# Row transfers of a mixture-of-experts layer paced by the tile, and moved inside the attention before it

## The chip, the cores and the metric

The kernel runs on one core of a Trainium2 chip. A core has five engines that run on their own and wait for each other by semaphores: TensorE (PE in the profile; its weight loads are shown as PEld), VectorE (DVE), ScalarE (ACT), GpSimd (POOL) and SyncE (SP), which here only issues transfers. Transfers move data between the core's on-chip memory and DRAM. Those with addresses taken from a table (indirect ones) are issued by GpSimd, all the others in this part by SyncE. Each engine and each issuing queue works in the order in which its instructions stand.

The metric is the device time of one execution in microseconds, as the median of several runs.

## The reference

Eight layers in a row, each followed by a residual addition and a layer norm: four attentions and four feed-forward networks ("ffn"), on a state of 8 blocks of 256 tokens with 256 features (seen as 2 x 128 or 4 x 64 tokens by some layers). Only the last two are touched.

The last attention, cut to its core (16 heads, two score maps each, their difference normalized again):

```python
energy = jnp.einsum('bqhad,bkhad->bahqk', qd, kd)
energy = jnp.where(causal, NEG, energy)
scores = jax.nn.softmax(energy / np.sqrt(D), axis=-1)
diff = scores[:, 0] - lam * scores[:, 1]
diff = jax.nn.softmax(jnp.where(causal, NEG, diff), axis=-1)
att = jnp.einsum('bhqv,bvhd->bqhd', diff, v)
```

The last ffn is a mixture of 32 experts; each token goes to the four with the largest routing weight:

```python
routing_weights = jax.nn.softmax(router_logits, axis=-1)
top_k_weights, top_k_indices = jax.lax.top_k(routing_weights, 4)
top_k_weights = top_k_weights / top_k_weights.sum(axis=-1, keepdims=True)
gate_up = jnp.einsum('TD,EDF->TEF', x, gate_up_proj)
g, u = jnp.split(gate_up, 2, axis=-1)
next_states = jnp.einsum('TEF,EFD->TED', u * jax.nn.silu(g), down_proj)
next_states = (next_states * router_weights[..., None]).sum(axis=1)
```

The kernel computes for each token only its four experts.

## The kernel before

**The last attention** (`attn3`, L537 to L847) works through 48 units: a block, a half of its 128-row query tiles, and one or two heads of each of four groups. A loop (L818) runs them as a pipeline with one unit in each stage. Its body, in the order in which it hands out instructions:

- `factors` of the unit before (L652): DVE takes reciprocals of the sums; GpSimd masks the diagonal of the first softmax (L661) and makes the factor `c` (L666, L667);
- a step of the queue `others` (L830);
- `scores` of this unit (L618): PE products, DVE maxima `nm` (L643), ACT exponentials `e` (L646);
- `values` of the unit three back, and steps of the next block's projections;
- `differences` of the unit before (L671), in two halves: DVE combines the two maps (`e`, L680, with `c`) and takes the maximum `nmd` (L684); GpSimd scales `nmd` (L685) and makes `v` (L688);
- a second step of `others` (L842);
- `turned` of the unit two back (L694): PE transposes its `v` (L705), ACT takes the exponential `p` (L707).

**The queue `others`** holds one generator, `ffn3_sort` (L1877), put there when the fourth block is normed (L799). It routes the first group of tokens of the next layer (the tokens come in two groups of four blocks, `GROUPS`): logits, top four, a slot for every pair of token and expert (`place`, L850), and then `scatter` (L931): 32 indirect transfers issued by GpSimd, each of 128 token rows of 1 KB from `X` to their slots in the DRAM tensor `rows` of the group. Between steps the generator yields. Behind the transfers it yields after two of three (L1923), so that a step issues one or two.

**The last ffn** (`ffn3`, L2037) runs `ffn3_experts` once for each group. The sorted rows are cut into 63 tiles of 128, each belonging to one expert (L31). For tile j the pipeline of L1996 does, one iteration each: `turn` (PE transposes the rows `xg`, DVE copies them to `xTg`), `up` (PE product with the expert's gate and up weights, ACT `sg`, DVE product `h`), `turn_back` (PE transposes `h`, ACT copies it to `hT`), and eight iterations after `turn` (`LAG`) `down` (PE product, ACT copy to `yg`). The expert's number is read into a register of PE. SyncE fetches three tiles of rows at a time, six tiles ahead (`fetch`, L1934, four buffers), and stores three tiles of results to the DRAM tensor `outs` (L1987, two buffers of `yg`). SyncE's order in this part is laid out by a scheduler's own model; the four computing engines keep the order in which the code hands out instructions.

While the first group's tiles run, `ffn3` works off what the attention left (L2054: one step every three tiles) and then one step a tile of `ffn3_sort` for the second group, with its 32 row transfers. While the second group's tiles run, it takes one step a tile of `ffn3_combine` (L2003) for the first group: for each 128 tokens, four indirect gathers of 128 result rows from `outs` into `yk` by GpSimd (L2019), four multiply-adds on DVE (`rk`, L2025, two 128-token tiles behind the gathers), and for every two tiles the norm: moments on DVE, `rsq` and `rstd` on GpSimd (L145, L146), the normalization on DVE (L189), and the store of the block. When all tiles are done, `ffn3_combine` runs for the second group with nothing beside it.

Of the kernel before, what the change touches and what calls it, by code (L numbers as in the profile page):

```python
# [10 lines left out]
F32 = mybir.dt.float32  # L11
# [7 lines left out]
P = 128  # L19
# [14 lines left out]
LAG = 8  # L34
# [5 lines left out]
class Model:  # L40


    def __init__(self, ctx, tc, ins, out):
        self.tc, self.nc, self.ins, self.out = tc, tc.nc, ins, out
        nc = self.nc
        self.const = ctx.enter_context(tc.tile_pool(name="const", bufs=1, side="left"))
        self.small = ctx.enter_context(tc.tile_pool(name="small", bufs=4, side="left"))
        self.psum = ctx.enter_context(
            tc.tile_pool(name="psum", bufs=2, space=bass.MemoryType.PSUM)
        )  # L50
        self.n_ev = 0
        self.rows, self.outs = (
            [
                nc.dram_tensor(f"{x}{g}", (n * P, D), F32, kind="Internal").ap()
                for g, n in enumerate(TILES)
            ]
            for x in ("rows", "outs")
        )
        self.lrows, self.louts = (
            [  # L60
                nc.dram_tensor(f"{x}{g}", (n * P, d), F32, kind="Internal").ap()
                for g, n in enumerate(TILES0)
            ]
            for x, d in (("lrows", ROW0), ("louts", P))
        )
        self.left = []
        self.sorted, self.sorted0 = {}, {}

        c = self.const
        self.X = [c.tile([P, 2, D], F32, name=f"X{b}", tag=f"X{b}") for b in range(NB)]  # L70
        self.xT = [c.tile([P, 2, BLK], F32, name=f"xT{k}", tag=f"xT{k}") for k in range(NBLK)]
        self.ident = c.tile([P, P], F32, name="ident")
        nc.sync.dma_start(out=self.ident, in_=ins["c_ident"])
        self.load_x(0, 2)

        self.tri = c.tile([P, 2 * P], F32, name="tri")
        self.identb = c.tile([P, P], BF16, name="identb")
        nc.vector.tensor_copy(self.identb, self.ident)
        self.maskA = c.tile([P, 4, P], BF16, name="maskA")
        self.one32 = c.tile([P, 32], F32, name="one32")  # L80
        nc.vector.memset(self.one32, 1.0)
        self.nhalf = c.tile([P, 16], F32, name="nhalf")
        nc.gpsimd.memset(self.nhalf, -0.5)
# [453 lines left out]
    def attn3(self, w, act, keep, start=False, beside=None):  # L537
# [5 lines left out]
        nc = self.nc  # L543
# [258 lines left out]
        others = []  # L802
# [15 lines left out]
        for n in range(len(units) + 3):  # L818

            def at(back):  # L820
                return units[n - back] if 0 <= n - back < len(units) else None

            u, last = at(0), at(1)
            if u and u.qc == 0 and u.h0 == 0:
                step(projections, 100)
                if u.b + 1 < NB:
                    projections.append(project(u.b + 1))
            if last:
                last.factors()
            step(others)  # L830
            if u:
                u.scores()
            if at(3):
                at(3).values()
            step(projections)
            halves = last.differences() if last else iter(())
            next(halves, None)
            step(projections, 2 if u and u.qc == 0 else 1)
            step(ends)
            next(halves, None)  # L840
            next(halves, None)
            step(others)  # L842
            if at(2):
                at(2).turned()
            ends += done
            done.clear()
# [1027 lines left out]
            gup=self.load(pool, "f3_gup", [P, 32, 2, 192], split=8),  # L1874
        )

    def ffn3_sort(self, w, g, act):  # L1877

        nc = self.nc
        first, n = GROUPS[g]
        n *= 2
        lg = self.ps("t")[:, : n * 32].rearrange("p (t e) -> p t e", e=32)
        for t in range(n):
            for c in range(2):
                nc.tensor.matmul(
                    lg[:, t, :], self.xt(first + t // 2, t % 2, c), w["gate"][:, c, :],
                    start=(c == 0), stop=(c == 1),  # L1890
                )
        nm = act.tile([P, n], F32, tag="r_nm", name="r_nm", bufs=1)
        nc.vector.tensor_reduce(nm, lg, AX.X, ALU.max)
        pr = act.tile([P, n, 32], F32, tag="r_pr", name="r_pr", bufs=1)
        nc.vector.tensor_tensor(
            pr, lg, nm.unsqueeze(2).to_broadcast([P, n, 32]), ALU.subtract
        )
        nc.scalar.activation(pr, pr, AF.Exp)
        yield
        top = act.tile([P, n, 8], F32, tag="r_top", name="r_top", bufs=1)  # L1900
        idx = act.tile([P, n, 8], U32, tag="r_idx", name="r_idx", bufs=1)
        for t in range(n):
            nc.vector.max(top[:, t, :], pr[:, t, :])
            nc.vector.max_index(idx[:, t, :], top[:, t, :], pr[:, t, :])
            if t % 4 == 3 or t == n - 1:
                yield
        one, slots, ends = yield from self.place(w, act, self.const, f"f3{g}", idx[:, :, 0:4], n)
        rows = self.scatter(
            self.rows[g], slots, lambda t, k: self.X[first + t // 2][:, t % 2, :]
        )  # L1910
        next(rows)
        expert = yield from self.tile_experts(w, act, self.const, f"f3{g}", ends)

        wt = self.const.tile([P, n, 4], F32, tag=f"r_w{g}", name="r_w", bufs=1)
        sm = act.tile([P, n], F32, tag="r_sm", name="r_sm", bufs=1)
        nc.vector.tensor_reduce(sm, top[:, :, 0:4], AX.X, ALU.add)
        nc.vector.reciprocal(sm, sm)
        nc.vector.tensor_tensor(
            wt, top[:, :, 0:4], sm.unsqueeze(2).to_broadcast([P, n, 4]), ALU.mult
        )  # L1920
        self.sorted[g] = wt, slots, expert
        yield
        for i, _ in enumerate(rows):  # L1923
            if i % 3 != 0:
                yield

    def ffn3_experts(self, w, g, act):


        nc = self.nc  # L1930
# [23 lines left out]
        def up(j):  # L1954
            er[j] = nc.tensor.value_load(expert[0:1, j : j + 1], min_val=0, max_val=31)
            ps = self.ps("a")[:, :192]
            for c in range(2):
                nc.tensor.matmul(  # L1958
                    ps, xT[j][:, c, :], w["gup"][:, bass.ds(er[j], 1), c, :].rearrange(
                        "p o f -> p (o f)"  # L1960
                    ),
                    start=(c == 0), stop=(c == 1),
                )
            sg = act.tile([P, 96], F32, tag="sg", name="sg", bufs=3)
            nc.scalar.activation(sg, ps[:, 0:96], AF.Silu)
            h[j] = act.tile([P, 96], F32, tag="h", name="h", bufs=3)
            nc.vector.tensor_tensor(h[j], sg, ps[:, 96:192], ALU.mult)

        def turn_back(j):
            pt = self.ps("s")[:96, :P]  # L1970
# [22 lines left out]
        fetch(3)  # L1993
        if self.down is None:
            self.down = self.load(act, "f3_down", [96, 32, D], split=8)
        steps = ((0, turn), (1, up), (2, turn_back), (LAG, down))  # L1996
        for j in range(tiles + LAG):
            for i, f in steps:
                if 0 <= j - i < tiles:
                    f(j - i)  # L2000
            yield

    def ffn3_combine(self, g, act):  # L2003


        nc = self.nc
        first, n = GROUPS[g]
        wt, slots, _ = self.sorted[g]
        ys, rs = {}, {}
        for t in range(2 * n + 2):  # L2010
            i = t - 2
            b = first + i // 2
            if t < 2 * n:
                ys[t] = act.tile([P, 4, D], F32, tag="yk", name="yk", bufs=4)
# [22 lines left out]
    def ffn3(self, w, act, left, start=False):  # L2037
# [20 lines left out]
        for x in left:  # L2058
            for _ in x:
                pass  # L2060
        put = self.ffn3_combine(0, act)
        for _ in self.ffn3_experts(w, 1, act):
            next(put, None)
        for _ in put:
            pass
        for _ in self.ffn3_combine(1, act):
            pass


# [1 line left out]
def tile_layers(ctx: ExitStack, tc: tile.TileContext, ins, out, phases):  # L2071
    m = Model(ctx, tc, ins, out)
    sides = ("left", "right")
    stack = {}
# [23 lines left out]
    for i, name in enumerate(phases):  # L2098
        m.last = i == len(phases) - 1
        with tc.tile_pool(name=f"act{i}", bufs=2, side=sides[i % 2]) as act:  # L2100
# [4 lines left out]
            with tc.manual_schedule(engines=engines) if name in MANUAL else ExitStack():  # L2105
# [10 lines left out]
                elif name == "attn1":  # L2116

                    def then(i=i):
                        keeps[i - 1].close()
                        open_weights(i + 1)  # L2120

                    m.attn1(w, act, left, then, start=start)
                elif name == "attn3":
                    beside = None
                    if not m.last:
                        beside = partial(m.ffn3_sort, stack[i + 1][1], 0)
                    left = m.attn3(w, act, kept[i], start=start, beside=beside)
                elif name == "ffn3":
                    m.ffn3(w, act, left, start=start)
                    keeps[i - 1].close()  # L2130
                else:
                    getattr(m, name)(w, act, start=start)
# [126 lines left out]
```

## Time and profile before

| | us |
|---|---|
| median of 3 runs (2551.92 to 2557.06) | 2555.08 |
| the profiled execution | 2616.84 |
| its span | 2615.1 |
| PE busy in the span | 2245.8 |
| DVE busy | 1433.7 |
| ACT busy | 1043.8 |
| GpSimd busy | 891.6 |

The profile is of one execution. The last attention lasts from about 1775 to 2253 us in it, the tiles of the first group from 2258 to 2421, those of the second from there to 2554, and the rest is the last combine. Time is given from the start of the span. A transfer that GpSimd issues is shown as an instruction of GpSimd; those of SyncE are shown as SPq. In a timeline, the bracket says how long the engine was idle before the instruction and what ended that; "remote" is a release that the profile cannot name. The sum of the engines' busy times says little here, since the stages have different limits.

### The profile page before, as it was taken

The numbers are of one execution on the slowest core, as the hardware profiler recorded it, in microseconds if no ns is written. First come the engines' busy times: TensorE is split into PE (matmuls) and PEld (weight loads), VectorE is DVE, ScalarE is ACT, GpSimd is POOL, SyncE is SP. The second block draws the span as 40 slices with busy tenths as digits, with TensorE's granted clock in tenths as the row PEclk, the third lists the DMA queues.
The fourth block names the chain that finished last, engine by engine and source line by source line (L and its number), as shares of the span: only waits on it lengthen the run. The fifth ranks groups of instructions, "written<-read, shape, count | busy, mean of one in ns | idle before, by whom it ended". The sixth has DMA issues, their size and how long they took to land.

```text
span 2615.1 us, 35980 instructions
## 1 busy us (share of the span) xinstructions
PE 2245.8 (86%) x12016; PEld 1522.2 (58%) x12016; DVE 1433.7 (55%) x3597; ACT 1043.8 (40%) x3001; POOL 891.6 (34%) x1599
## 2 busy tenths in 40 slices
PE   8998889899999999999999999898877866677790
PEld 4554688756666666666654565455555644455570
DVE  4655286754544544543474354656888886442353
ACT  1233355453543543534431112214776556433240
POOL 1222234343433332332222220004666558431315
PEclk9998999999999999999999999998989887788795
DMA  5000411100001000000520101002000001434453
GB/s 153 1 1 1 154 37 45 45 20 4 4 3 35 17 1 1 1 1 1 196 73 0 49 1 50 1 1 99 1 1 1 2 9 41 119 125 148 148 161 98
DMA packets 92306, 120.74 MB, mean 46 GB/s; under 512 B 9757, under 2 KB 79582, under 8 KB 91102
## 3 DMA queue, kind: packets, MB, share of 16 engines
q1 hardware_dynamic: 82270, 95.75, 11.4%
q0 software_dynamic: 8192, 21.11, 2.5%
q8 instruction: 100, 1.64, 0.3%
q10 hardware_dynamic: 1664, 1.57, 0.2%
q14 instruction: 80, 0.66, 0.1%
HBM read 67.53 MB, written 50.88 MB: 45 GB/s over the span
## 4 chain that ended last, share of the span: by engine, by line
PE 25%; DVE 11%; POOL 7%; issue 3%; ACT 2%; DMA 1%; another core or an unknown queue 1%; POOLq 0%; SPq 0%; DVEq 0%; ACTq 0%
PE ps_a L1958 4%; DVE e L680 2%; PE ps_a L1579 2%; PE ps_o L1977 2%; PE ps_s L1579 2%; POOL v L688 2%; PE ps_o L1830 2%; PE ps_a L1783 2%; PE ps_s L1783 2%; DVE nm L643 1%; DVE nmd L684 1%; POOL yk L2019 1%; PE ps_t L1950 1%; DVE bnst L182 1%; POOL rows L937 1%
## 5 line engine op out<-in xcount | busy, mean ns | idle before, releaser
L1370 POOL TENSOR_SCALAR p<-p,rs 128x128 f32<-128x128 f32 (+1 forms) x256 | 104.2, 424 | 293.6 <-DVE rs L1368 289.2
L145 POOL TENSOR_SCALAR rsq<-bnmv 128x2 f32<-128x2 f32 x64 | 13.7, 214 | 516.3 <-DVE bnmv L183 508.9
L1360 ACT ACTIVATE p<-ps_s,nm,rq 128x128 f32<-128x128 f32 (+1 forms) x256 | 127.9, 506 | 151.2 <-DVE nm L1358 151.1
L1288 ACT ACTIVATE sq<-ps_a 128x512 f32<-128x512 f32 x126 | 76.0, 603 | 227.9 <-PE ps_a L1280 227.7
L1958 PE MATMUL ps_a<-w_f_gup,xTg 128*128 x504 | 119.2, 363 | 40.8 <-DVE xTg L1952 20.8
L646 ACT ACTIVATE e<-ps_a,nm 128x128 f32<-128x128 f32 (+1 forms) x256 | 105.8, 436 | 110.9 <-DVE nm L643 95.6
L688 POOL TENSOR_SCALAR v<-e,r,nmd 128x128 f32<-128x128 f32 (+1 forms) x256 | 135.4, 540 | 10.0
L1289 DVE TENSOR_REDUCE ssk<-sq 128x4 f32<-128x512 f32 x64 | 43.8, 686 | 172.4 <-ACT sq L1288 172.4
L1280 PE MATMUL ps_a<-w_a_wq,xT 128*128 128x512 f32 x256 | 123.6, 606 | 11.7 <-DVE k L1302 9.2
L705 PE MATMUL ps_t<-ident,v 128*128 128x128 f32 x384 | 69.9, 319 | 69.0 <-DVE qT L584 31.4
L680 DVE SCALAR_TENSOR_TENSOR e<-e,c 128x128 f32<-128x128 f32 (+1 forms) x256 | 106.1, 463 | 34.6 <-POOL c L667 34.4
L1280 PE MATMUL ps_a<-w_a_wv,xT 128*128 128x512 f32 x256 | 121.4, 596 | 2.1 <-ACT q L1313 2.1
L1958 PEld LDWEIGHTS ps_a<-w_f_gup,xTg 128*128 128x128 f32 x504 | 88.4, 210 | 53.0 <-issue 28.5
L1280 PE MATMUL ps_a<-w_a_wk,xT 128*128 128x512 f32 x248 | 116.5, 593 | 0.0
L1289 DVE TENSOR_REDUCE ssq<-sq 128x4 f32<-128x512 f32 x64 | 43.9, 686 | 131.9 <-ACT sq L1288 131.9
L1408 PE MATMUL ps_o<-w_a_wo,attT 128*128 128x256 f32 x512 | 111.8, 379 | 0.0
L646 ACT ACTIVATE e<-ps_s,nm 128x128 f32<-128x128 f32 (+1 forms) x256 | 106.8, 453 | 0.0
L1408 PEld LDWEIGHTS ps_o<-w_a_wo,attT 128*128 128x128 f32 x512 | 96.7, 190 | 12.8
L705 PEld LDWEIGHTS ps_t<-ident,v 128*128 128x128 f32 x384 | 50.2, 163 | 89.4 <-POOL nmd L685 44.9
L1144 DVE SCALAR_TENSOR_TENSOR yg<-ps_t,xg,yg 128x128 f32<-128x128 f32 x266 | 93.0, 350 | 13.6 <-PE ps_t L1133 2.9
L1347 PE MATMUL ps_s<-kT,qT 128*128 128x256 f32 (+1 forms) x512 | 99.5, 327 | 0.0
L2019 POOL DMA_INDIRECT yk<-outs,r_slots x64 | 62.2, 973 | 108.3 <-DMA outs<-yg 89.9
(402 smaller groups left out, 6127.5 us busy)
## 6 DMA issues: line engine op xcount, KB each, us to landing
rows<-zero SPq DMA_DIRECT2D x42, 384.0 KB
xg<-rows SPq DMA_DIRECT2D x42, 384.0 KB
outs<-yg SPq DMA_DIRECT2D x42, 384.0 KB
w_f_gup<-in_f_gup SPq DMA_DIRECT2D x8, 768.0 KB
w_f_w<-in_f_w SPq DMA_DIRECT2D x8, 512.0 KB
w_f_down<-in_f_down SPq DMA_DIRECT2D x8, 384.0 KB
w_f_up<-in_f_up SPq DMA_DIRECT2D x5, 512.0 KB
lrows<-zero SPq DMA_DIRECT2D x12, 204.0 KB
```

Of the source, the lines that this page charges most:

```text
L646: nc.scalar.activation(e[:, s, j * nk : (j + 1) * nk], sc[s][:, j, :], AF.Exp, bias=nm[:, s, j : j + 1], scale=1.0, accum_out=sums[:, s, j ...
L680: nc.vector.scalar_tensor_tensor(d[:, s, h, :], u.e[:, s, h, 1, :], u.c[:, s, h : h + 1], d[:, s, h, :], ALU.mult, ALU.add,)
L688: nc.gpsimd.tensor_scalar(u.v[:, s, h, :], d[:, s, h, :], u.r[:, s, h, 0:1], nm[:, s, h : h + 1], ALU.mult, ALU.add,)
L705: nc.tensor.transpose(ps[:, s, c, :], x, self.ident)
L1280: nc.tensor.matmul(ps, self.xt(u.b, t, c), w[which][:, c, u.cols], start=(c == 0), stop=(c == 1),)
L1347: nc.tensor.matmul(sc[:, j, :], u.qT[:, h0 + j, qc * P : (qc + 1) * P], u.kT[:, h0 + j, 0:nk], start=(j == 0), stop=False,)
L1360: nc.scalar.activation(u.p[qc][:, h0 + j, :], sc[:, j, :], AF.Exp, bias=nm[:, j : j + 1], scale=r[:, j : j + 1], accum_out=u.sums[qc][:, h ...
L1370: nc.gpsimd.tensor_scalar(u.p[qc][:, j, :], u.p[qc][:, j, :], ri[:, j : j + 1], 1.0, ALU.mult, ALU.mult,)
L1408: nc.tensor.matmul(y[:, t, :], attTs[b][:, h, t * P : (t + 1) * P], w["wo"][:, h, :], start=(h == 0), stop=(h == 15),)
L1579: nc.tensor.matmul(x, xT[:, c, tok], w[name][:, c, cols], start=(c == 0), stop=(c == 1),)
L1783: nc.tensor.matmul(x, w[name][:, c, cols], xT[:, c, :], start=(c == 0), stop=(c == 1))
L1958: nc.tensor.matmul(ps, xT[j][:, c, :], w["gup"][:, bass.ds(er[j], 1), c, :].rearrange("p o f -> p (o f)"), start=(c == 0), stop=(c == 1),)
```

## The change

Six edits, all for the last two layers:

1. In the attention's loop, the second step of `others` (behind the differences) becomes two steps, but is left out while `ffn3_sort` is at its row transfers (a flag, `scattering`).
2. `ffn3_sort` yields after each row transfer, or, in the attention, after every third (`each=3`). Those of the first group so stand three in a row behind the factors.
3. Each `up` gets a copy of one element of `h` on GpSimd (`beat`): GpSimd's queue cannot pass it before that tile's `h` is there. `h` has four buffers instead of three. With one step of the sort a tile, one transfer stands between two beats.
4. In the second group `down` comes four iterations after `turn`, instead of eight.
5. `ffn3_combine` of the first group starts at the second group's iteration 8 instead of 0, with one step, so at most one gather, an iteration.
6. The last `ffn3_combine` lets its multiply-adds trail the gathers by one 128-token tile instead of two.

```diff
             next(halves, None)
             next(halves, None)
-            step(others)
+            if not self.scattering:
+                step(others, 2)
...
-    def ffn3_sort(self, w, g, act):
+    def ffn3_sort(self, w, g, act, each=1):
...
         self.sorted[g] = wt, slots, expert
+        self.scattering = True
         yield
         for i, _ in enumerate(rows):
-            if i % 3 != 0:
+            if i % each == each - 1:
                 yield
+        self.scattering = False
...
-            h[j] = act.tile([P, 96], F32, tag="h", name="h", bufs=3)
+            h[j] = act.tile([P, 96], F32, tag="h", name="h", bufs=4)
             nc.vector.tensor_tensor(h[j], sg, ps[:, 96:192], ALU.mult)
+
+            beat = act.tile([1, 1], F32, tag="beat", name="beat", bufs=2)
+            nc.gpsimd.tensor_copy(beat, h[j][0:1, 0:1])
...
         if self.down is None:
             self.down = self.load(act, "f3_down", [96, 32, D], split=8)
-        steps = ((0, turn), (1, up), (2, turn_back), (LAG, down))
-        for j in range(tiles + LAG):
+            lag = LAG
+        else:
+            lag = 4
+        steps = ((0, turn), (1, up), (2, turn_back), (lag, down))
+        for j in range(tiles + lag):
...
-    def ffn3_combine(self, g, act):
+    def ffn3_combine(self, g, act, ahead):
...
-        for t in range(2 * n + 2):
-            i = t - 2
+        for t in range(2 * n + ahead):
+            i = t - ahead
...
-        put = self.ffn3_combine(0, act)
-        for _ in self.ffn3_experts(w, 1, act):
-            next(put, None)
+        put = self.ffn3_combine(0, act, 2)
+        for j, _ in enumerate(self.ffn3_experts(w, 1, act)):
+            if j >= 8:
+                next(put, None)
         for _ in put:
             pass
-        for _ in self.ffn3_combine(1, act):
+        for _ in self.ffn3_combine(1, act, 1):
             pass
...
-                        beside = partial(m.ffn3_sort, stack[i + 1][1], 0)
+                        beside = partial(m.ffn3_sort, stack[i + 1][1], 0, each=3)
```

More of the change, by code (lines that the diff above doesn't have):

```diff
@@ L1921, in ffn3_sort @@
         self.sorted[g] = wt, slots, expert
+        self.scattering = True
         yield
         for i, _ in enumerate(rows):
-            if i % 3 != 0:
+            if i % each == each - 1:
                 yield
+        self.scattering = False
     def ffn3_experts(self, w, g, act):
```

## The prediction

> **What bounds the kernel now.** The page first: span, tenths by slice, granted clock, chain.
>
> ```profile
> span 2615.1 us, 35980 instructions
> ...
> PE   8998889899999999999999999898877866677790
> ...
> PEclk9998999999999999999999999998989887788795
> ...
> PE 25%; DVE 11%; POOL 7%; issue 3%; ACT 2%; DMA 1%; another core or an unknown queue 1%; POOLq 0%; SPq 0%; DVEq 0%; ACTq 0%
> ```
>
> TensorE is nearly full through slice 27. The change touches only the last attention and the last ffn (from 1775 us), where PE drops to 6 or 7 tenths and the clock with it. So second, busy time by stretch (columns: stretch, length, busy us and counts of PE, PEld, DVE, ACT, POOL, clock, DMA share, GB/s):
>
> ```profile
> 2147.00:2200.00 53.00, 37.95 (x292) 25.27 (x290) 36.82 (x79) 32.89 (x133) 42.07 (x81) 0.74 0.11 38
> 2200.00:2252.00 52.00, 29.10 (x192) 17.28 (x192) 29.81 (x65) 23.50 (x74) 42.03 (x81) 0.75 0.11 39
> ...
> 2340.00:2360.00 20.00, 4.05 (x12) 2.43 (x10) 0.68 (x2) 1.25 (x4) 15.12 (x17) 0.50 0.29 104
> 2360.00:2380.00 20.00, 10.31 (x42) 8.26 (x43) 3.72 (x11) 3.75 (x15) 5.73 (x6) 0.60 0.39 125
> 2380.00:2400.00 20.00, 18.33 (x113) 15.73 (x111) 8.20 (x25) 9.61 (x38) 0.00 (x0) 1.00 0.53 158
> ```
>
> In the attention's last 105 us, with row transfers on POOL, POOL is the fullest engine. In the ffn PE sets the pace (113 matmuls in 20 us), except while POOL issues 32 transfers in a row (2326.96 to 2366.29): 12 matmuls in 20 us. The waits of the attention's stretch (who waited for whom, total, times, longest) and the timeline inside the stall:
>
> ```profile
> DVE e L680 <- POOL c L667: 27.8, 10, 6.6
> ```
>
> ```profile
> 2351.29 0.64 PE L1950 MATMUL ps_t<-ident,xg 128*128 128x128 f32 x2
> ...
> 2355.89 0.37 ACT L1985 COPY yg<-ps_o 128x256 f32<-128x256 f32 x1 [3.94 <-remote]
> 2360.10 0.42 DVE L1952 COPY xTg<-ps_t 128x256 f32<-128x256 f32 x1 [9.97 <-remote]
> ...
> 2360.67 0.66 PE L1958 MATMUL ps_a<-w_f_gup,xTg 128*128 x1 [8.75 <-DVE xTg L1952]
> ```
>
> PE's two transposes end at 2351.93 by the record, yet DVE's copy of them starts 8.2 us later; once DVE is done, PE follows in 0.15 us. Only what comes from PE is late. Last, the chain and the timeline of the tail:
>
> ```profile
> 2546.91 0.67 PE ps_a L1958 x4
> ...
> 2549.42 2.49 DMA outs<-yg
> ...
> 2553.55 2.52 DMA outs<-yg
> ...
> 2556.89 1.03 POOL yk L2019
> ```
>
> ```profile
> 2598.31 0.95 POOL L2019 DMA_INDIRECT yk<-outs,r_slots  x1 [0.30 <-issue]
> ...
> 2600.36 0.74 DVE L189 TENSOR_SCALAR X<-rk,bnmv,rstd 128x256 f32<-128x256 f32 x2 [5.54 <-POOL rstd L146]
> ...
> 2603.48 1.53 DVE L2025 SCALAR_TENSOR_TENSOR rk<-yk,r_w,rk 128x256 f32<-128x256 f32 x3
> ```
>
> After the last gather DVE still has eight combines, since it sat in a normalization that waited behind all gathers.
>
> **The stall may belong to the recording.** This decides the forecast. An undisturbed tile takes 1.6 us (timeline: the copies xTg of tiles 40 to 60). Tiles 30 to 39 take 49.7 us, 35 too many; tiles 69 to 75, beside 16 gathers, 25.7 us, 16 too many; tiles 84 to 102 some 13 too many. Together 64 us. The profiled execution took 2616.84 us, the median is 2555.08: 61.8 less. PE-bound slices leave little room for that difference elsewhere. I take the stall to be mostly absent from the unprofiled runs: an inference, not shown.
>
> **What the Trainium skill says.** "Perfetto Trace Analysis", section "Summary: the profiler window per engine type": the end of a TensorE window is an estimate. The trace agrees: 8.2 us between the recorded end and the reader's start. Same page, "DMA Instruction — SWDGE (GPSIMD)": such a transfer's window ends when descriptors are written, not when data has moved. Agrees: windows of 0.95 us, while the first gather of the tail (2556.89) has its reader at 2559.83. "DMA: Bandwidth & Descriptors", "Issuing engines are not separate DMA queues": transfers of POOL and SP run on the same 16 engines. The trace shows room: DMA share 0.29 in the stall, 0.53 in full flow. "TensorE: Matmul & The Clock Gate", "What's actually happening": an idle window of about 3.4 us halves the clock; here 0.50 at 2340 to 2360. So each stall also costs slow matmuls afterwards, included in the excess.
>
> **The change, part by part** (against the profiled execution, less its stalls).
>
> *Sort and rows of group 0.* The twelve or so sort steps run three a unit, not two; the same DVE, PE and ACT work stands denser. The 31 remaining transfers stay three a unit but all stand between the factors and the differences; before, one stood there and two behind the differences, delaying the next unit's c: the 27.8 us over ten units. That is not the gain. POOL is busy 84.1 of 105 us; its fixed gaps (0.30 us after a transfer, 0.07 after others) take 11, two waits for ACT's table work 3.7; about 3 us can go. Three in front delay nmd and v by up to 2 x 1.26 us, but PE turns v one unit later (turned acts on the unit before last), which covers it. By the order of instructions the last transfer stands more than a unit earlier, so the last unit, without projections, runs free of three: some 1 to 2 us. Denser sorting could cost 1 to 3. I take -4 (bounds -8 to +4).
>
> *Start of the ffn.* On SP the first load of w_f_down stood ahead of the first xg (2253.33, then 2253.96); now both xg stand ahead: -0.6.
>
> *The beat.* 126 copies of one element on GpSimd (the order of instructions shows transfers and beats alternating, so the change does what it says); nearest row rsq, 128x2, 0.19 us. It waits for h; behind it in POOL's queue stand the tile's transfer, the last block's asq, ms, att and rstd, and the sort's two fills; DVE waits for rstd a tile later, and for a beat four tiles back before it overwrites h (hence four buffers, not three). A tile costs POOL 0.2 + 0.2 gap + 1.0 = 1.4 of 1.6 us: covered, at nothing. Without cover (a beat of 0.5 us or more) 31 tiles would grow by 0.1 to 0.2 us each, +5. Bounds 0 to +5; I take 0.
>
> *Rows of group 1.* Before, unprofiled, 32 transfers take 40 us from tile 30 and land at about tile 56. SP's first fetch of group 1 stands behind the store of tile 39 and waits for them, from tile 53 on; behind it stands the store of tile 42, whose buffer tile 48 needs at step 56: about 2 us of stall. After, one a tile from tile 30, the last goes at step 62 and lands 4 us later. The fetch now stands between the stores of tiles 51 and 54. The store of tile 54 went at 2417.56, 3.7 us after step 62 began, so it is held about 0.7 us, and the first fetch lands just as the drain ends (2421.1): +1.2. Together -0.8 (bounds -4 to +5).
>
> *Lag 4 in group 1.* Before, 5.97 us lie between the last product's end (2547.58) and the last store (2553.55), 2.5 of them a wait for a yg buffer. After, only sg, h, turn back, hT, down, yg: about 2.4 us from the chain's rows (0.26 + 0.26 + 0.31 + 0.26 + 0.7 + 0.38 and gaps): -3.5. Four downs move into the first tiles, at some 0.3 us each (1.6 against 1.35): +1.3. Net -2.2.
>
> *Gathers of group 0 from tile 8, one a tile.* 48 steps end at 55 of 67: hidden beneath the tiles, 0. If not all fitted they would land on the tail at 1.25 us each.
>
> *Ahead 1 in the tail.* A third rstd now stands before the last gather: +0.96 (a rstd between gathers: 2577.97 less 2576.71, less 0.30). Gather at 2599.3, lands 2.6 us later, one combine of 0.48: done at 2602.4, not 2605.0. POOL's rstd finds its moments ready: four gathers take 5.0 us, landing and moments about 3.5. Net -2.5. For group 0 it stays 2.
>
> Sum: -4 -0.6 -0.8 -2.2 -2.5 = -10.1. From the median: 2545. The after profile should fall further, to about 2560 to 2575, since the recording's stall shrinks.
>
> **Rivals.** *The stall is real.* For: it stands in the trace, and one transfer a tile thins it. Against: the 61.8 us, and that only PE's handoffs are late while DMA is at 0.29. Pace falls only from 1.26 to 1.6 us a transfer, so half to three quarters of 64 us go: -32 to -48 more, about 2505. *Hidden anyway.* POOL saturated, the ffn PE-bound, the tail's gains given back by denser sorting: 2553. *Slower: late v in the attention.* If PE cannot absorb the 2.5 us by which v is late, because POOL is full, each unit grows. One transfer's 1.26 us exposed in ten units is +12.6 in place of -4: with the other -6.1, 2562; both exposed, 2574. It decides from 1.1 us a unit (6.1 + 5.1 over ten). For: PE already waits for POOL's v and nmd in this stretch; against: POOL's order only trades the place of the same work.
>
> **How the numbers follow.** No change can be told within 0.2%, 5.1 us. My forecast 60% (own range 2535 to 2554), stall real 13%, hidden 10%, slower 17%. Faster: 0.77 of the 60 and the 13, 0.60; same: most of the rest of the 60 and the 10, 0.20; slower 0.20. The range 2520 to 2564 holds nearly all of the first and third and half of the slower case; it leaves out most of the real stall.
>
> **What would show it.** DVE's wait for c L667 nearly gone and POOL's share unchanged in the attention's end; rows<-X alternating with beat in the ffn; the tile near 1.6 us through it; about 2.4 us from the last product to the last store; one combine after the last gather. If the median falls by over 30 us, I was wrong about the stall; if units with transfers exceed 10.3 us, about v; if DVE's h waits for a beat, about the cover.

## The result and the profile after

The changed kernel takes 2540.09 us (median of six runs, 2532.27 to 2542.09), the kernel before 2554.18 (six runs): a ratio of 0.9942, 95% interval 0.9926 to 0.9959. By the medians it is 14.1 us faster, by the ratio 14.8 (10.5 to 18.9), where 10.1 were forecast. The profiled execution took 2540.15 us against 2616.84; its span fell by 76.7 us, five times what the runs show. That gap is taken up below. One run of all those told of here, of a version without the beat, took 2932.54 us at a granted clock of 0.735 where the others of its kernel had 0.944 to 0.947; no ratio counts it.

The page of the changed kernel: span, tenths by slice, granted clock.

```profile
span 2538.4 us, 36327 instructions
...
PE   8998979989999999999999999998887787668990
...
PEclk9998999999999999999999999999998978789995
```

The slices that dropped to 6 and 7 tenths while the tiles ran are gone; what stays low is the attention's end and the start of the ffn. Busy time by stretch of the changed kernel: two stretches of the attention with row transfers, then two of the first group's tiles with the second group's transfers (columns as in the prediction: stretch, length, busy us and counts of PE, PEld, DVE, ACT, POOL, clock, DMA share, GB/s):

```profile
2130.00:2182.00 52.00, 35.77 (x292) 24.72 (x291) 39.35 (x88) 34.54 (x134) 43.51 (x85) 0.87 0.12 41
2182.00:2234.00 52.00, 36.84 (x258) 22.17 (x258) 35.60 (x79) 30.53 (x113) 43.88 (x90) 0.67 0.11 39
...
2318.00:2346.00 28.00, 26.43 (x162) 22.77 (x160) 12.63 (x40) 13.72 (x54) 18.57 (x33) 1.00 0.69 218
2346.00:2372.00 26.00, 24.57 (x146) 20.81 (x146) 10.35 (x31) 13.39 (x52) 18.96 (x34) 1.00 0.60 206
```

GpSimd is busy for 87.4 of 104 us in the attention's end, before 84.1 of 105. Beside the transfers PE now has 162 matmuls in 28 us and 146 in 26 us, where the profile before had 12 in 20 us. GpSimd's timeline there:

```profile
2352.00 0.98 POOL L939 DMA_INDIRECT rows<-X,r_slots  x1 [0.16 <-issue]
2352.99 0.18 POOL L1974 COPY beat<-h 1x1 f32<-1x1 f32 x1
2353.32 0.98 POOL L939 DMA_INDIRECT rows<-X,r_slots  x1 [0.16 <-issue]
2354.31 0.18 POOL L1974 COPY beat<-h 1x1 f32<-1x1 f32 x1
```

Transfers and beats alternate, a beat takes 0.18 us. The waits over the same attention stretch (who waited for whom, total us, times, longest), and the chain of the drain and the timeline of the tail:

```profile
DVE e L681 <- POOL c L668: 16.0, 8, 6.1
```

```profile
2474.86 0.90 PE ps_a L1962 x4
...
2478.43 0.38 ACT yg L1992
2478.81 0.02 issue
2478.83 2.51 DMA outs<-yg
```

```profile
2524.95 0.96 POOL L2029 DMA_INDIRECT yk<-outs,r_slots  x1 [0.30 <-issue]
...
2527.84 0.48 DVE L2035 SCALAR_TENSOR_TENSOR rk<-yk,r_w,rk 128x256 f32<-128x256 f32 x1 [0.84 <-DMA yk<-outs,r_slots]
```

The wait for c is down from 27.8 to 16.0 us, not gone as forecast. From the last product of `up` to the last store it is 3.07 us (2475.76 to 2478.83) instead of 5.97, and each of the last combines now waits for its own gather: one is left behind the last.

### The profile page after: what moved, and what is told of

It is laid out like the page before. It is cut to its first block, busy times and chain, and to the rows that moved or that the text cites. A ratio compares the mean times of both kernels' runs of the same rounds, so it can differ in the third digit from the quotient of the medians.

```text
span 2538.4 us, 36327 instructions
## 1 busy us (share of the span) xinstructions
PE 2225.3 (88%) x12016; PEld 1510.7 (60%) x12016; DVE 1432.9 (56%) x3597; ACT 1044.6 (41%) x3001; POOL 916.3 (36%) x1725
## 5 line engine op out<-in xcount | busy, mean ns | idle before, releaser
L1962 PE MATMUL ps_a<-w_f_gup,xTg 128*128 x504 | 112.2, 347 | 10.8 <-DVE xTg L1956 4.2
L1146 DVE SCALAR_TENSOR_TENSOR yg<-ps_t,xg,yg 128x128 f32<-128x128 f32 x266 | 93.1, 350 | 12.5 <-PE ps_t L1135 3.6
L1396 PE MATMUL ps_o<-pT,V 128*128 128x256 f32 x256 | 79.5, 392 | 19.3 <-ACT pT L120 19.2
L1962 PEld LDWEIGHTS ps_a<-w_f_gup,xTg 128*128 128x128 f32 x504 | 83.0, 198 | 21.3 <-ACT yg L1992 10.7
```

The source lines that it names most:

```text
L1146: nc.vector.scalar_tensor_tensor(acc[j], y, c, acc[j], ALU.mult, ALU.add)
L1962: nc.tensor.matmul(ps, xT[j][:, c, :], w["gup"][:, bass.ds(er[j], 1), c, :].rearrange("p o f -> p (o f)"), start=(c == 0), stop=(c == 1),)
```

## The experiments

The twelve runs went in three groups of four, each group with its own runs of the kernel before on the same chip. By their records the three groups ran on three different chips, called A, B and C here. On A and B the kernel before takes 2553.21 and 2550.87 us, on C 2615.84. Where a difference in us stands with an interval, it is the ratio less one, times the median of the kernel before in the same group. That the times depend so much on the chip is the largest finding, so it is told first.

### The stall of the profile before

> The kernel before, recorded once more, nothing changed. If every recording of it stalls TensorE beside the 32 transfers in a row: a span near 2615 us again, with tiles 30 to 39 in some 50 us. If the stall was a chance of that one execution (three other kernels with the same row of 32 transfers have shown none): a span of 2548 to 2558 us, tiles 30 to 39 in 14 to 15 us, and 18 to 21 us from tile 57 to tile 63, where SyncE's queue is held by the first fetch of the second group.

It took 2552.45 us, its span is 2550.7 (chip B). Its stretches beside the row of 32 transfers:

```profile
2325.00:2345.00 20.00, 19.07 (x118) 16.42 (x116) 9.56 (x32) 9.70 (x39) 15.12 (x17) 1.00 0.73 237
2345.00:2365.00 20.00, 18.79 (x116) 16.34 (x115) 8.57 (x25) 9.61 (x37) 15.24 (x16) 1.00 0.76 255
```

GpSimd issues as densely as in the first profile (16 or 17 instructions, 15.1 to 15.2 us busy in 20), and PE runs 116 to 118 matmuls where the first profile had 12. So neither the row of transfers nor the recording is enough for the stall: of the two cases expected the numbers are the second's. Then chip C:

> The changed kernel once more, on one chip with the two versions below, which it was not compared with directly. About 0.994 of before; the profile as the first one within 6 us.

Before: 2612.14 to 2619.30 us in all 11 runs there. The changed kernel: 2553.94, ratio 0.9758 (0.9742 to 0.9773), 63.3 us faster, so the expected 0.994 was missed by far. And without the beat:

```diff
-            beat = act.tile([1, 1], F32, tag="beat", name="beat", bufs=2)
-            nc.gpsimd.tensor_copy(beat, h[j][0:1, 0:1])
```

> The changed kernel without the beat; all else stays. If the pacing costs what it cost alone (3.4 us): about 2536 to 2537 us. If the wait at the boundary of the groups only changes its place (in the traces so far 5.5 us over the undisturbed tiles without pacing, 5 with it): within 2 us of the changed kernel, 2538 to 2542. If pacing keeps TensorE from a stall that is real: 30 us or more slower.

On chip B: 2534.66 us, ratio 0.9942 (0.9925 to 0.9958) to before, the same ratio as the changed kernel's in its own comparison. So nothing is seen there that the beat buys; whether it costs the 3.4 us of the first case or nothing, these two comparisons cannot tell.

> The changed kernel without the beat, on the same chip as the changed kernel. If the pacing costs what it cost alone: 2 to 4 us below the changed kernel. If it only moves the wait at the boundary: within 1 us of it.

On chip C the same kernel: 2597.94 us, ratio 0.9935 (0.9922 to 0.9948). The changed kernel beside it is 44 us faster. This expectation missed it; the one of the run on B had named it, as the case of a real stall. The stretches of the version without the beat on C:

```profile
2321.00:2341.00 20.00, 12.59 (x55) 9.60 (x55) 4.88 (x19) 3.45 (x13) 15.22 (x16) 0.81 0.50 169
2341.00:2361.00 20.00, 3.06 (x10) 2.05 (x9) 0.68 (x2) 0.89 (x3) 15.12 (x17) 0.50 0.41 140
```

and of the changed kernel on C:

```profile
2325.00:2345.00 20.00, 18.49 (x112) 15.73 (x110) 8.64 (x26) 9.27 (x37) 12.97 (x24) 1.00 0.69 231
2345.00:2365.00 20.00, 16.32 (x96) 13.63 (x95) 7.17 (x22) 8.50 (x33) 12.68 (x22) 0.98 0.65 211
```

The stall, with PE down to 10 matmuls in 20 us, is there without the beat and nearly gone with it. It looks as in the first profile. The ffn of the kernel before shows it on C as well, in a version that changes only the attention (the third one under "The attention", attn_flip):

```profile
2334.00:2354.00 20.00, 5.10 (x14) 3.24 (x14) 0.93 (x3) 0.82 (x4) 15.11 (x17) 0.50 0.40 143
```

In the timeline of the version without the beat on C, the transposes end at 2341.25 by the record and DVE copies them at 2349.42:

```profile
2340.62 0.63 PE L1954 MATMUL ps_t<-ident,xg 128*128 128x128 f32 x2
...
2349.42 0.42 DVE L1956 COPY xTg<-ps_t 128x256 f32<-128x256 f32 x1 [9.95 <-remote]
...
2366.23 0.37 ACT L1989 COPY yg<-ps_o 128x256 f32<-128x256 f32 x1 [2.55 <-remote]
2366.27 0.42 DVE L1956 COPY xTg<-ps_t 128x256 f32<-128x256 f32 x1 [6.52 <-remote]
2366.50 0.26 ACT L1969 ACTIVATE sg<-ps_a 128x96 f32<-128x96 f32 x1
2366.64 0.26 ACT L1977 COPY hT<-ps_s 96x128 f32<-96x128 f32 x1
```

The last of the 32 transfers is issued at 2360.62. Some 5 us later the waiting reads of ACT and DVE follow each other at once; the products of the first two had ended at 2361.12 and 2361.56 by the record. PE's ends are estimates (see the prediction), so the trace cannot tell whether the products are late or only the word of them.

Time from one tile's xTg copy to another's, worked out from the timelines (us):

| tiles | before, first profile | before, B | without beat, B | without beat, C | changed, first profile | changed, C |
|---|---|---|---|---|---|---|
| 27 to 42 (row transfers) | 60.5 | 24.3 | 24.5 | 61.1 | 24.4 | 25.3 |
| 42 to 57 | 24.0 | 23.5 | 22.9 | 23.7 | 24.0 | 28.6 |
| 57 to 66 (groups meet) | 18.2 | 22.6 | 23.3 | 18.6 | 23.4 | 23.4 |
| 66 to 125 (gathers) | 121.4 | 91.6 | 90.0 | 114.5 | 89.7 | 95.8 |

The first profile of before agrees with C row by row (attn_flip, with the same ffn, has 61.0, 23.1, 18.5 and 119.7 us there), and its total (2616.84) lies inside C's runs. So it was most likely taken under the conditions of C, and the three timed runs shown with it were not: that it was C itself no record says.

On C the stall costs the version without the beat 56 us between tile 0 and tile 125 (281.7 against 225.6) and the changed kernel 10 (236.9 against 226.7).

Only the beat was taken out, so that it removes most of the stall is shown. How it does so is argued. It can work as a brake that PE holds: it waits for the tile's h, so a late tile delays the next transfer, and on C the 32 transfers are spread over 58.9 us, in the first profile of after over 52.9, by the same code. But on C the transfers also come thinner with it, 1.87 us from one start to the next on average, where they came every 1.27 us without. Whether thinning alone would do no run tells: a beat that waits for nothing was not tried.

(Medians of different chips are compared here only between A and B, where the kernel before agrees within 0.1%. Stretches are compared more widely: the attention's ten units with transfers take 106.3 us in the first profile of before and 106.7 on A and B, so there they agree; the four sorting units less so, 53.2, 55.5 and 52.5.)

Why PE's results come late on C beside GpSimd's transfers, and whether it is the chip or the conditions of that time, stays open: each chip was met once.

### The attention

```diff
-            step(others)
+            if not self.scattering:
+                step(others, 2)
...
-            if i % 3 != 0:
+            if i % 3 == 2 if each == 3 else i % 3 != 0:
                 yield
```

> Only the attention's part of the change (two sort steps behind the differences; the first group's transfers three in a row behind the factors). Theory (GpSimd is full here, the gain comes from sorting and transfers that end earlier, so the last unit runs free of them): the median falls by 5 to 9 us, and the profiled execution by about as much, with the stall in the ffn still in the profile (near 2605). Rival (the late v costs what the earlier c gives, and the 10 us between the two profiles are chance): within 3 us of before. Rival (placing the transfers ahead of the differences is the gain, since DVE no longer waits for c): the units with transfers get shorter by 1 us or more, and the median falls by over 9 us.

2543.52 us, ratio 0.9961 (0.9948 to 0.9974) on A: -10.0 us (-13.3 to -6.6). The median is that of the second rival (over 9 us), though the units with transfers got 0.7 us shorter and not 1 (table below). The profiled execution took 2543.76 us, with no stall, where 2605 were expected. Then the denser sort without moving the transfers:

```diff
-            step(others)
+            step(others, 1 if self.scattering else 2)
```

> The sort in the attention runs three steps a unit instead of two, the transfers keep their places of before (one behind the factors, two behind the differences). If the earlier end makes the attention's gain: as much as the attention's whole part, 5 to 9 us. If the placement of the transfers makes it: 0 to 2 us.

2554.27 us, ratio 1.0005 (0.9993 to 1.0016), so nothing that can be told. The placement makes the gain. One more run asks how many transfers have to stand in front; the kernel before with one more yield ahead of them has two in front and one behind:

```diff
         yield
+        if g == 0:
+            yield
         for i, _ in enumerate(rows):
```

> The kernel before with one step more ahead of the first group's transfers, so that two of three stand in front of the differences and one behind them (before: one and two; the change: three and none). If the attention's gain is the wait of GpSimd for DVE's nmd, which transfers in front fill: two fill it nearly whole (that wait from 4.2 to 4.5 us in eight units to under 1.5), and the median falls by 6 to 9 us. If the gain goes with the number of transfers that c no longer waits for: half of it, 4 to 6 us. If only three in a row do it: within 2 us of before.

On C: 2606.31 us, ratio 0.9969 (0.9957 to 0.9981), -8.1 us (-11.2 to -5.0). The interval leaves open which of the first two cases it is; the traces decide. The attention by units, each counted from GpSimd's first `v` in the second half of `differences`, and the last stretches from and to the start of GpSimd's last mask (us):

| units | before, B | attention of before, A (tail_alone, below) | attn_dense, A | attn_alone, A | attn_flip, C |
|---|---|---|---|---|---|
| 4, sorting | 52.5 | 55.5 | 57.8 | 57.8 | 53.3 |
| 10, with transfers | 106.7 | 106.7 | 108.1 | 99.7 | 100.1 |
| to the last mask | 12.7 | 12.6 | 8.9 | 7.7 | 11.0 |
| last mask to tile 0's copy | 14.8 | 15.4 | 13.1 | 12.6 | 16.4 |

Denser sorting costs 2.3 us in its own units and 1.4 in the next ten (columns of A), and gets 3.7 and 2.3 back in the last stretches. With two or three transfers in front a unit takes 10 us, with one 10.7 to 10.8. Eight of these units in the kernel before on B: first the stretch, then its waits.

```profile
2142.00:2228.40 86.40, 56.12 (x427) 36.46 (x428) 59.48 (x126) 51.84 (x196) 69.01 (x134) 0.77 0.11 38
```

```profile
DVE e L680 <- POOL c L667: 17.1, 7, 3.7
...
POOL rows L937 <- issue: 5.0, 24, 0.3
...
POOL nmd L685 <- DVE nmd L684: 4.5, 11, 1.1
```

The same eight with the attention's part alone:

```profile
2143.40:2223.70 80.30, 53.34 (x429) 34.27 (x430) 58.03 (x126) 52.02 (x196) 66.51 (x134) 0.80 0.12 40
```

```profile
DVE e L681 <- POOL c L668: 9.0, 6, 2.9
...
POOL rows L939 <- issue: 6.0, 23, 0.3
```

and, with two in front:

```profile
DVE e L680 <- POOL c L667: 9.4, 5, 2.8
...
POOL rows L937 <- issue: 4.9, 23, 0.3
```

GpSimd's wait for DVE's nmd (4.5 us, eleven times) is gone in both. Before, GpSimd came to the scaling of nmd with only one transfer in front, waited for DVE, and afterwards had two transfers to issue while DVE waited for the next c. With two in front it issues while DVE computes. Of the 6.1 us that eight units save with the attention's part alone, 3.6 are idle time of GpSimd (86.4 less 69.0, so 17.4 us, became 80.3 less 66.5, so 13.8) and 2.5 are busy time (69.0 to 66.5: v took 546 ns and now 512, asq 742 and 613). The first is about what the wait for nmd gives (4.5 us), less the 1.0 us that GpSimd idles more behind its transfers (5.0 to 6.0). Why v and asq got shorter stays open.

### The end

```diff
+        else:
+            lag = 4
-        steps = ((0, turn), (1, up), (2, turn_back), (LAG, down))
+        steps = ((0, turn), (1, up), (2, turn_back), (lag, down))
...
-        for _ in self.ffn3_combine(1, act):
+        for _ in self.ffn3_combine(1, act, 1):
```

> Only the lag of four iterations in the second group and multiply-adds one 128-token tile behind the gathers at the end. Theory: -2.2 for the drain and -2.5 for the last combines, so the median falls by 4.7 us (3 to 6); in the profile 2.4 to 3.5 us from the last product to the last store instead of 6, and one combine behind the last gather. Rival (the earlier downs give the drain's gain back): -2.5 us. The profiled execution keeps the stall, at 2600 to 2615.

2545.41 us on A, ratio 0.9968 (0.9957 to 0.9980): -8.2 us (-11.0 to -5.1). Its profiled execution took 2546.27 us, where 2600 to 2615 were expected: no stall again. From the last xTg copy to the end of the span it takes 64.0 us instead of 69.0. Much of the rest came from the tiles of the second group: 89.7 us from tile 66 to 125 instead of 91.6 (before, B) or 92.3 (attn_dense). Their first nine (66 to 75) got longer, 13.4 us instead of 12.4 and 12.5; those from 75 to 120 shorter, 68.9 us instead of 72.0 and 72.6. (The boundary, tiles 57 to 66, took 21.0 us instead of 22.6 and 23.8, though nothing was changed there.) PE's and its weight loads' waits for ACT there, first attn_dense, then this kernel:

```profile
PEld ps_a L1961 <- ACT yg L1988: 6.1, 11, 0.8
...
PE ps_a L1961 <- DVE rk L2028: 1.7, 5, 0.5
```

```profile
PE ps_a L1958 <- ACT yg L1985: 0.6, 3, 0.2
PEld ps_a L1958 <- ACT yg L1985: 0.4, 1, 0.4
```

With the shorter lag `up` hardly waits for ACT's `yg` any more. Why the lag changes that was not tested.

### The pacing and the boundary of the groups

```diff
+            beat = act.tile([1, 1], F32, tag="beat", name="beat", bufs=2)
+            nc.gpsimd.tensor_copy(beat, h[j][0:1, 0:1])
...
-            if i % 3 != 0:
+            if i % 3 != 0 or g:
                 yield
...
+            if j >= 8:
+                next(put, None)
```

> Only the beat, four buffers of h, one transfer a tile for the second group, and the first group's gathers from iteration 8. Theory (the stall of the profile before belongs to the recording): the median moves by -1 to +5 us, the profiled execution falls by 55 to 65 us, to within 8 us of its own median. Rival (the stall is real): the median falls by 30 us or more.

2556.64 us on A, ratio 1.0013 (1.0005 to 1.0021), +3.3 us (1.3 to 5.4); its profiled execution took 2560.11. Both numbers are as the theory had them, but not for its reason: on A the versions without the beat had no stall either, so none was there to remove. The trace finds little of the 3.3 us. Tiles 9 to 57 take 91.2 us against 90.0 and 89.9 in the two versions on A with the ffn of before (attn_dense, attn_alone), the boundary 23.1 against 23.8 and 23.7, tiles 66 to 125 92.5 against 92.3 and 92.4.

At the boundary every version loses time. In the version with the attention's part alone (no pacing), the store of results stands behind the fetch of the second group, which waits for its rows to land; ACT then waits for the store:

```profile
SPq L1943 <- DMA rows<-X,r_slots: 8.5, 4, 4.9
```

```profile
ACT yg L1989 <- DMA outs<-yg: 6.0, 2, 5.7
```

So the first fetches were given to GpSimd, behind its own transfers:

```diff
-            nc.sync.dma_start(
+            q = nc.gpsimd if g and j < 12 else nc.sync
+            q.dma_start(
```

> The changed kernel with the second group's first four fetches of rows issued by GpSimd, behind its own row transfers, so that SyncE's queue no longer waits for them in front of the stores of the first group. If that wait is what the pacing costs at the boundary: tiles 57 to 66 take some 18.5 us instead of 23.4, and the median is 4 to 6 us below the changed kernel, about 2535. If the tiles there wait for the rows themselves, the last of which goes at step 62: no gain, 2539 to 2541.

2538.41 us on B, ratio 0.9956 (0.9941 to 0.9972): no gain on the changed kernel's 0.9942 (which was measured beside other runs of before). Tiles 57 to 66 take 23.5 us, as in the changed kernel. With SyncE free PE waits for the rows themselves:

```profile
PE ps_t L1955 <- DMA xg<-rows: 3.2, 1, 3.2
```

> The same fetches by GpSimd, and no beat: the rows are all there before the boundary and the queue of stores is free. Theory: 5 us below the version without the beat, the best of all, 2532 to 2536. If the pacing by itself costs nothing, the same as with the beat, within 1 us.

2533.22 us on B, 0.9925 (0.9907 to 0.9943). That is in the expected range, but 1.4 us below the version without the beat and not 5, and the intervals of the two overlap (0.9925 to 0.9958 there). Tiles 57 to 66 take 21.9 us instead of 23.3, not the 18.2 to 18.6 seen where the rows had landed long before; what still holds them was not worked out.

> Without the beat and with the second group's first four fetches by GpSimd. If it is the best version: 3 to 7 us below the changed kernel, the interval apart from 0.994 of before.

On C: 2597.93 us, 0.9932 (0.9916 to 0.9948), the same as without the fetches by GpSimd, and 44 us slower than the changed kernel instead of 3 to 7 faster. No version is shown to beat the changed kernel everywhere: without the beat it is at best a few us faster on B, with it 44 us on C.

## Why the prediction was right, and where its steps were not

**The stall.** The conclusion (absent from the timed runs, so 2545 and not 2505) held. Its step "the stall may belong to the recording" fell: on C all timed runs of before are as long as the first profile, and the ffn of before has the stall in attn_flip's trace; on B a recording has none. That the forecast held is luck in this: nothing in it named the conditions of the timed runs, and had these been C's, the change would have been worth 63 us. The reading that failed is taking the difference of profile and runs for a cost of recording; it was a difference of conditions. The rival "the stall is real" is what happens on C: it promised 32 to 48 us more, and C shows 63.3 in place of 14.8, 48.5 more. Its argument "pace falls only from 1.26 to 1.6 us a transfer" is neither shown nor refuted: on C it fell from 1.27 to 1.87, and the wait for h was never tried apart from the pace. The 8.2 us were also read as agreeing with an end that is only an estimate. Without the stall the copy follows the same kind of end at once (in the first profile after, transposes end at 2473.61 and their copy starts at 2473.64), so the 8.2 us belong to the stall.

**After profile at 2560 to 2575.** It took 2540.15, and 2555.1 on C. Wrong by the same step.

**Sort and rows in the attention, -4.** Measured -10.0 (-13.3 to -6.6), outside the bound of -8 by its middle. The step that failed is "that is not the gain", with "about 3 us can go". The sum behind it did not close: of 105 us GpSimd was busy 84.1, the gaps took 11 and two waits 3.7, which leaves 6.2 us and not 3. The waits of the same stretch name most of them:

```profile
POOL nmd L685 <- DVE nmd L684: 5.1, 13, 1.1
```

This wait of GpSimd for DVE is what the transfers in front fill, and nothing in the sum held it. The denser sort alone comes to nothing that can be told (+1.3, -1.8 to 4.1). It costs 2.3 us in its own units, inside the 1 to 3 of the sum; the stretch to the last mask, free of most transfers, gives 3.7, where 1 to 2 were forecast. The late v, the slower rival, did not show: units with transfers got shorter.

**Start of the ffn, -0.6.** SyncE's order changed as forecast: the first two fetches of xg (2243.35) now stand ahead of w_f_down (2244.30). From the start of the last mask to tile 0's copy 14.8 us (before, B) became 12.4, but tiles 0 to 9 went from 21.7 to 23.5: -0.6 in net. Neither 2.4 nor 1.8 was in the forecast, so that the net agrees is chance.

**The beat, 0, and the rows of group 1, -0.8.** Together +3.3 (1.3 to 5.4). The cover held (one wait of h for a beat, 0.6 us); with the pacing alone tiles 27 to 57 are 0.5 to 0.7 us longer than in the three versions on A without it (49.2 against 48.5 to 48.7). The boundary takes 22.6 us (before, B) and 23.4 (changed). Where the stall makes the rows land long before, it takes 18.2 to 18.6, so the hold is about 4 and 5 us, an estimate from these, instead of the sum's 2 us and 1.2 us. In the changed kernel the rows hold it as well as the stores: with the stores' queue free PE waits for rows (3.2 us), and nothing is gained. Where most of the 3.3 us goes is open.

**Lag 4, -2.2.** The drain shrank from 5.97 to 3.07 us, -2.9 against -3.5. The step "four downs move into the first tiles, +1.3" held: tiles 66 to 75 got 1.0 us longer. What the sum lacked are the tiles after them, 3.1 us shorter from 75 to 120, in the stretch where the waits of `up` for `yg` are nearly gone.

**Ahead 1, -2.5.** From the last store to the end of the span 61.6 us (before, B) became 59.6: -2.0.

The sum was -10.1, the medians say -14.1. With each part measured alone, the attention with the start of the ffn was 5.4 us too small and the end 3.5, the pacing 4.1 us too good. So the number came within 4 us because misses of both signs offset each other. The three parts alone add up to -14.9, as much as the whole change by its ratio (-14.8).

## What to carry to other kernels

Where a shared engine alternates between serving another engine and issuing transfers, put the transfers where it would wait for that other engine; two in the right place were worth about as much as three. Before calling a difference between a profile and the timed runs a cost of recording, record the same kernel again: here a second recording had no stall, and a third chip had it in the timed runs. A tiny instruction that makes the issuing engine wait for the consumer's progress came, with the rest of the pacing, at some 3 us here, and saved 44 where the transfers disturbed.

## What the runs showed of the hardware

The same kernel takes 2551 to 2553 us on two chips and 2616 on a third. Most of the difference is a stall in which TensorE's results reach their readers up to 8 us late, by the recorded ends, while GpSimd issues indirect transfers 1.27 us apart; DMA share is 0.29 to 0.50 in it, 0.73 to 0.76 in the same stretch where it doesn't occur. A copy of one element on GpSimd that waits for each tile's result removes 46 of its 56 us. The mean granted clock (0.931 to 0.934 in the profiles with the stall, 0.942 on B) differs by 1% and doesn't explain it, since the tiles outside the bursts take the same time (23.7 and 22.9 us for tiles 42 to 57 without the beat).
